# A graph network's two layers on one core: products from block 12, another order on PE and ACT, 28 early tiles

## The chip, the cores and the metric

The kernel runs on one core of a Trainium2 chip. The time is the device time of one execution in microseconds (us); the runs shown are 3 of the kernel before, 3748.28 to 3751.44 with a median of 3750.68. One more execution was taken by the hardware profiler; every row that is quoted comes from it. The engines are named as in the profile: PE multiplies matrices (PEld is its loading of weights), DVE is the vector engine, ACT the scalar engine with its table of functions, POOL the engine that issues the indirect gathers here, SP the one that issues the other DMAs.

## What is computed

A graph has 6250 nodes with 128 features and 200000 edges, sorted by their end (dst). Two layers, each added to its input:

```python
def _L0_gnn_ref(feat, src, dst, W, attn_l, attn_r, bias):
    z = (feat @ W).reshape(N, HEADS, PER_HEAD)          # 8 heads of 16
    el = jnp.einsum('nhp,hp->nh', z, attn_l)
    er = jnp.einsum('nhp,hp->nh', z, attn_r)
    e = jax.nn.leaky_relu(el[src] + er[dst], negative_slope=NEG_SLOPE)
    emax = jax.ops.segment_max(e, dst, num_segments=N)
    a = jnp.exp(e - emax[dst])
    denom = jax.ops.segment_sum(a, dst, num_segments=N)
    agg = jax.ops.segment_sum(z[src] * a[:, :, None], dst, num_segments=N)
    out = agg / jnp.maximum(denom, 1e-09)[:, :, None]
    ...

def _L1_gnn_ref(node_feats, edge_attrs, edge_feats, ...):
    s, v = ...                                          # up projections of the nodes
    h = silu(edge_feats @ A1 + b1); h = silu(h @ A2 + b2); tpw = h @ A3
    ss, vs = s[sender], v[sender]
    ...                                                 # four kinds of messages of 128 + 384 numbers
    message = jax.ops.segment_sum(mji, receiver, num_segments=num_nodes) / 10.0
    ...                                                 # output projections

h = maximum(layernorm(x), 0);  x = x + _L0_gnn_ref(h, ...)
h = maximum(layernorm(x), 0);  x = x + _L1_gnn_ref(h, ...)
```

## The kernel before

**Tiles, blocks, steps.** The edges lie in 1563 tiles of 128, the tiles in NB = 98 blocks of KB = 16 (the last has 11), each block for a window of 64 nodes. The nodes lie in NX = 50 tiles of 128. In each layer every edge needs the row of its source node out of a table in DRAM (t0, 136 numbers, for layer 0; t1, 128 numbers, for layer 1). Nearly all these rows come by indirect DMAs of POOL, one per tile of 128 edges (`gather`, L836 to L839). The exceptions:

- Column 15 of each third block comes by 128 DMAs of one row each, from SP (`rows_by_row`, L1141 to L1155); they are issued far ahead, between SP's other requests.
- Column KD = 14 of the blocks in `dense` (layer 0) or `dense1` (layer 1) is made by PE: the table lies on the chip as three bf16 parts (t0s, t1s), a one-hot matrix of the sources picks the rows by 51 products of up to 408 columns (`rows_of`, L1304), and `taken` (L1317) lays the result in place. `dense` before is blocks 21 to 93 (L1200).
- The first KX = 25 tiles of layer 0 are gathered from the raw input x while t0 is still being made (`gather_x`, L903), and put through the same arithmetic again (`rows_of` of the prologue, L938, called a second time).
- The first NE = 24 tiles of layer 1 ("early") are gathered from a copy of t1 that lacks the last three node tiles, so that POOL needn't wait for them at the seam between the layers; the missing rows are added in layer 1 by one-hot products (`late_ends`, L1863, and `late_rows`, L1877).

**The prologue** (L845 to L1005) normalizes the 50 node tiles in ten groups, multiplies by W, and writes t0. Of its subtract-and-scale operations (L960) five are given to POOL, the rest to DVE and ACT.

**Layer 0's loop** (L1577 to L1669) has one step g for each block g. PE, DVE, ACT and SP execute in the order in which the program writes their instructions, so that the order of the calls is the order of the queues. Step g works on four blocks: it ends block g−2, weights and sums block g−1 (b4), takes the logits of block g, and prepares block g+1 (n1: turning the one-hot ends, er of the ends) and g+2 (n2: one-hot ends, the products of a dense block). The calls that the change touches:

- `turned(n1, q)`, L1339: four transpositions of four one-hot tiles into p_d, which is one buffer of PSUM, and a copy d by ACT (L1348). The next turning waits for that copy.
- `er_of(n1, q)`, L1350: four small products that read d.
- `weights(b4)`, L1401: three operations of DVE, an exp on ACT (L1411), a transposition on PE (L1412), a copy on ACT (L1413). In odd steps ACT loads its function table ahead of the exp, since the node steps of even steps use a root.
- `weighted(b4, k0)`, L1416: DVE multiplies eight tiles of rows by their weights. `sums(b4, k0)`, L1425: PE adds them up by end, one product a tile, half a block a call.
- `rows_of(n2, k0, n)`: three products for each of n parts.
- `asked(k)`, L1262: SP requests three node tiles of t0 into zr, two buffers. `split(k)`, L1277: DVE makes their three parts, four operations (L1228 to L1231). Step g asks for g−2 and, at its end, splits g−3; 17 of each are needed.

The rows of block g+3 are requested in step g, and five buffers go round.

**Layer 1** (L1966 on) works in units of four tiles, 16 × 24 + 7 = 391 with the last block's 4, 4 and 3: edge network, messages, sums; then the nodes; at the end comes a tail for the last two node tiles.

Of the kernel before, what the change touches and what calls it, by code (L numbers as in the profile page):

```python
# [13 lines left out]
OP = mybir.AluOpType  # L14
# [727 lines left out]
def tile_even_edges(  # L742
# [60 lines left out]
    src_col = keep.tile([P, TU], I32, name="fsrc")  # L803
    z_first = keep.tile([P, KB, ZW], F32, name="fz_first")
    ok_i = keep.tile([1, 1], I32, name="fok")
    KX = KB + 9
    z_second = keep.tile([P, KB, ZW], F32, name="fz_second")
    other = keep.tile([P, KB, ZW], F32, name="fz_other")
    flat = other.rearrange("p k f -> p (k f)")
# [46 lines left out]
    with tc.manual_schedule(engines={mybir.EngineType.PE, mybir.EngineType.DVE,  # L856
# [81 lines left out]
        def rows_of(gx, xs, fp, fp_ps, raw=None):  # L938

            mark = "e" if raw else ""  # L940
            NC = len(gx)
            mvs, rss, mrs, hs = {}, {}, {}, {}
            todo, done, outs, ers = [], [], [], []
            for k in range(NC + 3):
                if 0 <= k - 1 < NC:
                    rss[k - 1] = deviation(fp, mvs[k - 1], gx[k - 1][1], f"x{mark}{gx[k - 1][0]}")
                c = k - 2
                if 0 <= c < NC:
                    i, n = gx[c]
                    rs, mr = rss[c], mrs[c] = normal(fp, mvs[c], rss[c], n, f"x{mark}{i}")  # L950
                    h = hs[c] = fp.tile([P, 6, P], F32, name="fh")
                    for j in range(n):
                        by = (i + j) % 7
                        if by in ((2, 6) if c < NC - 2 else (2,)):
                            nc.scalar.activation(h[:, j, :], xs[c][:, j, :], AF.Identity,
                                                 bias=mr[:, j, :], scale=rs[:, j, :])
                        else:
                            late = by in (0, 3, 5) and NC - 4 <= c < NC - 2 and not raw
                            eng = nc.gpsimd if late else nc.vector
                            eng.tensor_scalar(h[:, j, :], xs[c][:, j, :], mvs[c][:, j, 0:1],  # L960
                                              rs[:, j, :], op0=OP.subtract, op1=OP.mult)
                if k == NC + 1 and not raw:
                    uneven_edges()
                for i, n, zt in ers:
                    nc.vector.tensor_copy(er_all[:, i : i + n, :], zt[:, :n, ZW:])
                ers = []
                if k >= 3:
                    i, n = gx[k - 3]
                    zt = raw[k - 3] if raw else fp.tile([P, 6, CW], F32, name="zt", bufs=4)
                    todo += [(k - 3, zt, j0, min(3, n - j0)) for j0 in range(0, n, 3)]  # L970
                while todo:
                    c, zt, j0, m = todo.pop(0)
                    p_t = fp_ps.tile([P, 4, P], F32, name="p_t")
                    for j in range(m):
                        nc.tensor.transpose(p_t[:, j, :], hs[c][:, j0 + j, :], ident)
                    h_t = fp.tile([P, 3, P], F32, name="h_t")
                    nc.scalar.activation(h_t[:, :m], p_t[:, :m], AF.Relu)
                    done.append((c, zt, j0, m, h_t))
                    while len(done) > (1 if k < NC + 2 or todo else 0):
                        c, zt, j0, m, h_t = done.pop(0)  # L980
                        p_z = fp_ps.tile([P, 3, CW], F32, name="p_z")
                        for j in range(m):
                            nc.tensor.matmul(p_z[:, j, :], h_t[:, j, :], w_ext, start=True, stop=True)
                        outs.append((c, zt, j0, m, p_z))
                        while len(outs) > (1 if k < NC + 2 or todo or done else 0):
                            c, zt, j0, m, p_z = outs.pop(0)
                            copy = nc.scalar.copy if c < NC - 2 else nc.vector.tensor_copy
                            w = ZW if raw else CW
                            copy(zt[:, j0 : j0 + m, :w], p_z[:, :m, :w])
                            i, n = gx[c]  # L990
                            if j0 + m == n and not raw:
                                to_table(t0, zt[:, :, :ZW], i, n, nc.sync)
                                ers.append((i, n, zt))
                                load(c)
                if k < NC:
                    i, n = gx[k]
                    mvs[k] = moments(fp, xs[k], n, f"x{mark}{i}")
            for i, n, zt in ers:
                nc.vector.tensor_copy(er_all[:, i : i + n, :], zt[:, :n, ZW:])
# [11 lines left out]
def even_edges(tc, v):  # L1011
# [8 lines left out]
    with ExitStack() as ctx:  # L1020
# [25 lines left out]

        NL, NE = 3, 24
        LATE = NX - NL  # L1050
        sv_of = {}
        iota = const.tile([P, P], F32, name="fiota")
# [144 lines left out]
        order = sorted(range(NR), key=lambda k: (k > 0, 2 * NR + k < NX, k))  # L1197
        half = (NR + 1) // 2
        TS = 3
        dense = set(range(-(-NX // TS) + 4, NB - 4))  # L1200
        dense1 = set(range(10, NB - 4, 4))

        ranges = []
# [34 lines left out]
        with tc.manual_schedule(engines=in_order), \  # L1238
# [23 lines left out]
            def asked(k):  # L1262

                i = TS * k
                if 0 <= i < NX:
                    n = min(TS, NX - i)
                    zr = asked.of[k] = l0d.tile([P, TS, ZW], F32, name="zr", bufs=2)[:, :n]
                    if i == 0:
                        nc.vector.memset(zr[:W0, 0, :], 0.0)
                        nc.sync.dma_start(zr[W0:, 0, :], t0[: P - W0, :])  # L1270
                        of = t0[P - W0 : n * P - W0]
                        nc.sync.dma_start(zr[:, 1:], of.rearrange("(j p) f -> p j f", p=P))
                    else:
                        of = t0[i * P - W0 : (i + n) * P - W0]
                        nc.sync.dma_start(zr, of.rearrange("(j p) f -> p j f", p=P))

            def split(k):  # L1277
                if k in asked.of:
                    zr = asked.of.pop(k)
                    n = min(TS, NX - TS * k)  # L1280
                    in_three(t0s[:, TS * k : TS * k + n], zr, rest0[:, :n])
# [22 lines left out]
            def rows_of(c, k0, n):  # L1304

                if k0 == 0:
                    p_x = l0_ps.tile([P, 512], F32, name="p_x")
                    c["p_x"] = p_x[:, : 3 * ZW].rearrange("p (r f) -> p r f", f=ZW)
                for k in range(k0, min(k0 + n, NR)):
                    i = order[k]  # L1310
                    m = len(range(i, NX, NR))
                    for s in range(3):
                        nc.tensor.matmul(c["p_x"][:, :m, :], c["oh", k // half][:, k % half, :],  # L1313
                                         t0s[:, i::NR, s, :], start=k == 0 and s == 0,
                                         stop=k == NR - 1 and s == 2)
# [9 lines left out]
            def ends_of(c, q):  # L1325

                if 4 * q < c["kt"] and q == len(c.setdefault("s", [])):
                    c["s"].append(one_hot(c["b"] * KB + c["o"] + 4 * q, min(4, c["kt"] - 4 * q), iota_p))
# [21 lines left out]
            def er_of(c, q):  # L1350
                if 4 * q < c["kt"]:
                    b = c["b"]
                    er_w = (er3o if b % 2 else er3)[:, b // 2, :, :].rearrange("p s h -> p (s h)")
                    for k in range(min(4, c["kt"] - 4 * q)):
                        nc.tensor.matmul(er_3[:, 4 * q + k].rearrange("p s h -> p (s h)"),
                                         c["d", q][:, k, :], er_w, start=True, stop=True)
# [220 lines left out]
            for g in range(NG - 3):  # L1577
# [4 lines left out]
                    node_out(n)  # L1582
                for n in split_:
                    parts_out(n)
                asked(g - 2)
                if g % 2 == 0 and g // 2 + 2 < NX - 2:
                    node_rows(g // 2 + 2, 1)
                rows_until(rows, g + 1)
# [25 lines left out]
                er_of(n1, 0)  # L1614
                if was:
                    rows_of(n1, half + 4, NR)
                if b4:
                    weights(b4)
                if was:
                    taken(n1)  # L1620
                for n in nodes:
                    node_x(n)
                er_of(n1, 1)
                turned(n1, 2)
                if b4:
                    bank_of(b4)
                    weighted(b4, 0)
# [3 lines left out]
                er_of(n1, 2)  # L1631
                if b4:
                    weighted(b4, 8)
                if to:
                    rows_of(n2, 0, 3)
                for n in nodes:
                    node_d(n)
                    node_h(n)
                ends_of(n2, 2)
                er_of(n1, 3)  # L1640
                if b4:
                    sums(b4, 0)
                if to:
                    rows_of(n2, 3, 3)
                for n in nodes:
                    node_t(n)
                if n1 is not none:
# [6 lines left out]
                    sums(b4, 8)  # L1654
                if to:
                    rows_of(n2, 6, half - 6)
                split(g - 3)
                if g == 4:
                    ends_in_ranges(const)
                if g == NG - 4:  # L1660
# [74 lines left out]
        with tc.manual_schedule(engines=in_order), \  # L1735
# [192 lines left out]
            def dense_step(b, q):  # L1928
# [6 lines left out]
                if b in dense1:  # L1935
# [4 lines left out]
            blk = [{} for _ in range(NB)]  # L1940
            us = [{"b": b, "k0": k0, "m": min(4, KT[b] - k0)}
                  for b in range(NB) for k0 in range(0, KT[b], 4)]
            NU = len(us)

            def take_rows(b):
# [219 lines left out]
```

## Time and profile before

| | |
|---|---|
| runs: median (lowest, highest) | 3750.68 us (3748.28, 3751.44) |
| the profiled execution | 3749.37 us |
| its span, with the instructions | 3747.6 us |
| mean granted clock of PE | 0.936 |
| POOL, gathers of both layers (L839) | 2946, 0.945 us each |
| last gather from t0's table for layer 0 | block 97, ends at 1840.4 us |
| first gather from the complete t1 | 1876.60 us |
| last gather of layer 1 | ends at 3733.18 us |

How to read it: the page gives busy time by engine and by group of instructions; a timeline lists the instructions of one engine with start, duration, line, output and input, and in brackets the idle time ahead and what released it; the windows give each engine's busy time and PE's granted clock (1.00 is full speed) in a stretch. The page's chain that ended last is cut at the first steps of the end here, so that the pace of the two layers has to be read from the spacing of one line's instructions from block to block. PE's clock by fortieths of the span:

```profile
PEclk7766899999999999999799999999999999999999
```

### The profile page before, as it was taken

What the parts mean: (1) busy time and instruction counts of PE and PEld (TensorE: products, weight loads), DVE (VectorE), ACT (ScalarE), POOL (GpSimd) and SP (SyncE); (2) the same over time, 40 slices, a digit from 0 to 9 for tenths busy, and PEclk for the clock granted to TensorE, in tenths of its full rate; (3) what the DMA queues carried; (4) which work ended last, traced back from release to release, by engine and by line L of the source; (5) the groups of instructions that cost most, each with busy time, mean ns of one, the idle gap of its engine ahead of it and who ended that gap; (6) DMA issues with size and microseconds to landing.
All of it is one profiled execution on the core that took longest, in us unless ns stands there. A gap on an engine that the chain in (4) does not pass through costs nothing. (4 is left out here: it accounts for less than half of the span.)

```text
span 3747.6 us, 74803 instructions
## 1 busy us (share of the span) xinstructions
PE 3196.4 (85%) x19845; PEld 2474.1 (66%) x19845; DVE 2633.1 (70%) x6272; ACT 1406.0 (38%) x3638; POOL 2817.3 (75%) x2981
## 2 busy tenths in 40 slices
PE   4756788888888888888788899999999999999997
PEld 4655566666666666666666677777677777767775
DVE  7755666666666666666657777777777777777776
ACT  4432333333333333333334444444444444444443
POOL 7777777777777777777777777777777777777776
PEclk7766899999999999999799999999999999999999
DMA  6333332222222222222223222222222222222222
GB/s 167 75 78 79 71 68 67 68 69 68 68 68 68 68 68 67 69 69 67 71 70 95 69 64 64 64 64 64 64 64 64 65 63 64 65 63 64 63 68 52
DMA packets 212534, 262.78 MB, mean 70 GB/s; under 512 B 77425, under 2 KB 163921, under 8 KB 212097
## 3 DMA queue, kind: packets, MB, share of 16 engines
q0 software_dynamic: 95072, 200.78, 22.6%
q1 hardware_dynamic: 116592, 57.03, 5.7%
q8 instruction: 159, 2.61, 0.3%
q14 instruction: 279, 2.28, 0.2%
q10 hardware_dynamic: 432, 0.09, 0.0%
HBM read 236.19 MB, written 21.14 MB: 69 GB/s over the span
## 5 line engine op out<-in xcount | busy, mean ns | idle before, releaser
L839 POOL DMA_INDIRECT fz<-ft,fsrc x1750 | 1654.1, 945 | 539.5 <-issue 327.0
L1824 PE MATMUL p_u<-mj,s 128*128 128x256 f32 x3126 | 764.3, 388 | 87.5 <-DVE mj L1816 86.5
L1313 PE MATMUL p_x<-t0s,fz_first 128*128 128x408 bf16 (+1 forms) x3723 | 730.0, 346 | 0.0
L1824 PEld LDWEIGHTS p_u<-mj,s 128*128 128x128 f32 x3126 | 582.2, 192 | 215.6 <-DVE mj L1816 139.7
L839 POOL DMA_INDIRECT fz_other<-ft,fsrc x589 | 557.2, 946 | 179.6 <-issue 107.6
L839 POOL DMA_INDIRECT fz_second<-ft,fsrc x583 | 554.0, 950 | 178.3 <-issue 107.9
L1313 PEld LDWEIGHTS <-fz_first 128*128 128x128 bf16 x3723 | 361.5, 101 | 231.5 <-issue 17.4
L1791 ACT ACTIVATE p_w<-p_w,yb 128x64 f32<-128x64 f32 x1563 | 451.5, 289 | 117.3 <-PE p_w L1787 73.8
L1787 PE MATMUL p_w<-fa3p,h 128*128 128x256 f32 x1564 | 408.4, 384 | 0.0
L1787 PEld LDWEIGHTS p_w<-fa3p,h 128*128 128x128 f32 x1564 | 286.7, 193 | 114.5 <-issue 48.8
L1772 ACT ACTIVATE h<-p_h,fb 128x512 f32<-128x512 f32 x196 | 134.7, 687 | 585.8 <-PE p_h L1770 575.1
L1337 ACT COPY mk<-p_m 128x384 f32<-128x384 f32 (+1 forms) x99 | 47.4, 479 | 658.5 <-PE p_m L1333 651.6
L1427 PE MATMUL p_u<-fz,s 128*128 128x136 f32 x1846 | 272.9, 308 | 20.1 <-DVE fz L1422 20.1
L1427 PEld LDWEIGHTS p_u<-fz,s 128*128 128x128 f32 x1846 | 258.5, 216 | 23.8 <-DVE fz L1422 22.2
L1173 DVE TENSOR_TENSOR s<-p_i,fdloc 128x512 f32<-128x512 f32 x391 | 268.6, 687 | 3.8 <-ACT p_i L1766 3.8
L1173 DVE TENSOR_TENSOR s<-p_m,fdloc 128x512 f32<-128x512 f32 x391 | 266.2, 682 | 3.0 <-ACT mk L1337 2.7
L1770 PE MATMUL p_h<-ft,fa1p 128*128 128x128 f32 x1568 | 216.1, 282 | 56.5 <-DMA ft<-in_e_f_dram 56.3
L1770 PEld LDWEIGHTS p_h<-ft,fa1p 128*128 128x128 f32 x1568 | 208.7, 197 | 79.8 <-issue 55.7
L1348 ACT CAST d<-p_d 128x512 bf16<-128x512 f32 x391 | 229.3, 586 | 78.0 <-PE p_d L1346 34.2
L1378 DVE TENSOR_TENSOR_SCAN pe<-mk,pe 128x128 f32<-128x128 f32 x98 | 42.0, 428 | 290.8 <-PE pe L1293 271.6
L1777 ACT ACTIVATE h<-p_h,fb 128x512 f32<-128x512 f32 x196 | 134.7, 687 | 260.4 <-PE p_h L1774 260.4
L1811 DVE TENSOR_REDUCE vd<-vy 128x128 f32<-128x384 f32 x391 | 229.6, 587 | 0.0
(285 smaller groups left out, 4880.5 us busy)
## 6 DMA issues: line engine op xcount, KB each, us to landing
r<-ft SPq DMA_DIRECT2D x3968, 0.5 KB
r<-ft SPq DMA_DIRECT2D x3840, 0.5 KB
fz<-ft,fsrc POOLq DMA_INDIRECT x1750
fz_other<-ft,fsrc POOLq DMA_INDIRECT x589
fz_second<-ft,fsrc POOLq DMA_INDIRECT x583
fx<-x SPq DMA_DIRECT2D x47, 160.0 KB
ft<-in_e_f_dram SPq DMA_DIRECT2D x98, 64.0 KB
t1s<-fx SPq DMA_DIRECT2D x7, 576.0 KB
```

Source lines behind the costliest of these rows:

```text
L839: nc.gpsimd.indirect_dma_start(out=to[:, k, :width], out_offset=None, in_=table, in_offset=bass.IndirectOffsetOnAxis(ap=src_col[:, t : t + ...
L1173: nc.vector.tensor_tensor(s[:, :m], iota[:, None, :].to_broadcast([P, m, P]), dloc[:, t : t + m].unsqueeze(2).to_broadcast([P, m, P]), OP. ...
L1313: nc.tensor.matmul(c["p_x"][:, :m, :], c["oh", k // half][:, k % half, :], t0s[:, i::NR, s, :], start=k == 0 and s == 0, stop=k == NR - 1 ...
L1348: nc.scalar.copy(d[:, :m], p_d[:, :m])
L1427: nc.tensor.matmul(c["p_u"][:, :ZW], c["s"][k // 4][:, k % 4, :], c["z"][:, k, :], start=c["o"] + k == 0, stop=c["o"] + k == KT[c["b"]] - 1)
L1770: nc.tensor.matmul(p_h[:, q, :], a1p[:, q0 + q, :], c["ft"], start=True, stop=True)
L1772: nc.scalar.activation(c["h1"], p_h, AF.Silu, bias=b1)
L1777: nc.scalar.activation(h2, p_h, AF.Silu, bias=b2)
L1787: nc.tensor.matmul(w[:, k : k + n].rearrange("p k a u -> p (k a u)"), c["h2"][q // 4][:, q % 4, :], a3p[:, :n].rearrange("p k f -> p (k f) ...
L1791: nc.scalar.activation(w[:, k, ::2, :], w[:, k, ::2, :], AF.Copy, scale=c["yb"][:, k0 + k, 0:1])
L1811: nc.vector.tensor_reduce(vd, vy.rearrange("p t i u -> p t u i"), AX.X, OP.add)
L1824: nc.tensor.matmul(blk[b]["p_u"][:, :MW], u["s"][:, k, :], u["mj"][:, k, :], start=k0 + k == 0, stop=k0 + k == KT[b] - 1)
```

## The change

1. KX is KB + 13 = 29 in place of 25: four tiles more come from x, four fewer from t0.
2. All of L960's operations that POOL had go to DVE.
3. NE is 28 in place of 24.
4. `dense` begins at block 12 in place of 21.
5. Two parts of t0 are requested in each of the steps 2 to 10, and split at the end of the same step.
6. The order in a step: `er_of(n1, 1)` and `turned(n1, 2)` stand ahead of `weights(b4)`; the first three of the next dense block's parts stand ahead of `weighted(b4, 0)`, the second three ahead of the sums; the first half of the sums is parted, with `er_of(n1, 3)` between. On ACT the copy d of turning 2 so comes ahead of the table load and the exp. DVE's order is the same but for the splits.
7. The last unit of layer 1, of three tiles, becomes two of two and one.

```diff
-    KX = KB + 9
+    KX = KB + 13
...
-                            late = by in (0, 3, 5) and NC - 4 <= c < NC - 2 and not raw
-                            eng = nc.gpsimd if late else nc.vector
-                            eng.tensor_scalar(h[:, j, :], xs[c][:, j, :], mvs[c][:, j, 0:1],
-                                              rs[:, j, :], op0=OP.subtract, op1=OP.mult)
+                            nc.vector.tensor_scalar(h[:, j, :], xs[c][:, j, :], mvs[c][:, j, 0:1],
+                                                    rs[:, j, :], op0=OP.subtract, op1=OP.mult)
...
-        NL, NE = 3, 24
+        NL, NE = 3, 28
...
-        dense = set(range(-(-NX // TS) + 4, NB - 4))
+        dense = set(range(-(-NX // TS // 2) + 3, NB - 4))
...
-                asked(g - 2)
+                for k in range(2):
+                    asked(2 * g - 4 + k)
...
                 er_of(n1, 0)
                 if was:
                     rows_of(n1, half + 4, NR)
+                er_of(n1, 1)
+                turned(n1, 2)
                 if b4:
                     weights(b4)
                 if was:
                     taken(n1)
                 for n in nodes:
                     node_x(n)
-                er_of(n1, 1)
-                turned(n1, 2)
+                if to:
+                    rows_of(n2, 0, 3)
                 if b4:
                     bank_of(b4)
                     weighted(b4, 0)
...
                 er_of(n1, 2)
                 if b4:
                     weighted(b4, 8)
-                if to:
-                    rows_of(n2, 0, 3)
                 for n in nodes:
                     node_d(n)
                     node_h(n)
                 ends_of(n2, 2)
+                if to:
+                    rows_of(n2, 3, 3)
+                if b4:
+                    sums(b4, 0, 4)
                 er_of(n1, 3)
                 if b4:
-                    sums(b4, 0)
-                if to:
-                    rows_of(n2, 3, 3)
+                    sums(b4, 4, 4)
...
-                split(g - 3)
+                for k in range(2):
+                    split(2 * g - 4 + k)
...
+            if us[-1]["m"] > 2:
+                n = us[-1]["m"] - 2
+                us[-1]["m"] = 2
+                us.append({"b": NB - 1, "k0": us[-1]["k0"] + 2, "m": n})
```

## Prediction

> **What bounds the kernel now.** I read five views: the busy shares, the requests of POOL, the pace of layer 0 in PE's own order, PE's stalls in one pair of iterations (two successive blocks, 37.5 us), and the rows around the seam and the end.
>
> ```profile
> PE 3196.4 (85%) x19845; PEld 2474.1 (66%) x19845; DVE 2633.1 (70%) x6272; ACT 1406.0 (38%) x3638; POOL 2817.3 (75%) x2981
> ...
> L839 POOL DMA_INDIRECT fz<-ft,fsrc x1750 | 1654.1, 945 | 539.5 <-issue 327.0
> ```
>
> POOL is 75% busy, but each of its gathers takes 0.945 us and then 0.30 of issue, 1.2485 together, and 40 to 41 of them start in every 50 us from end to end. It never waits for a buffer. So a gather less is 1.2485 us less, wherever POOL sets the end. It pauses in two places only:
>
> ```profile
> 24.10 4.21 POOL L960 TENSOR_SCALAR fh<-fxs,mvx,rsx 128x128 f32<-128x128 f32 x5 [0.46 <-PE p_t L975]
> 28.47 1.03 POOL L905 DMA_INDIRECT fz_second<-in_e_xp_dram,frow  x1 [0.16 <-issue]
> ```
>
> ```profile
> 1869.61 0.94 POOL L839 DMA_INDIRECT fz<-ft1z,fsrc  x1 [0.31 <-issue]
> 1876.60 0.94 POOL L839 DMA_INDIRECT fz<-ft,fsrc  x1 [6.04 <-PE p_h L1868]
> ```
>
> The first is the prologue's arithmetic (next gather at 28.47 where it could be 23.94: 4.53 lost). The second is the seam: the first gather from t1 waits for layer 0's last table write, 6.04 where 0.30 is usual, 5.74 lost.
>
> PE follows the gathers in layer 0 until block 20 or so and then falls behind them: its logits come 2 us after the block's last gather at blocks 21 to 27, 27 to 30 us at 84 to 92. Its step of logits (L1372) stands at 253.25 for block 11, 429.96 for 20 and 1779.79 for 92, so (1779.79 − 429.96) / 36 = 37.50 a pair, where POOL needs 36.7 (2 × 14.67 gathers). The dense blocks, whose tile 14 PE makes itself (10.0 us of L1313 a block: 730.0 / 73), are thus bound by PE's loop, the others by POOL. Its stalls in one pair:
>
> ```profile
> 1188.54 0.33 PE L1412 MATMUL pe<-fident,a 128*128 128x128 f32 x1 [1.59 <-ACT a L1411]
> ...
> 1189.92 0.38 PE L1346 MATMUL p_d<-fidentb,s 128*128 128x128 bf16 x4 [0.73 <-ACT d L1348]
> ```
>
> ```profile
> 1207.58 0.38 PE L1346 MATMUL p_d<-fidentb,s 128*128 128x128 bf16 x4 [0.73 <-ACT d L1348]
> ...
> 1210.54 2.12 PE L1427 MATMUL p_u<-fz_other,s 128*128 128x136 f32 x16 [1.01 <-DVE fz_other L1422]
> ```
>
> In odd iterations PE waits 1.59 for the exp, because ACT loads its table first; in both 0.73 for the copy d of turned 2, since p_d is one buffer; in even ones 1.01 for DVE's weighted sums. And the clock dips:
>
> ```profile
> 1187.00:1190.40 3.40, 1.13 (x18) 0.94 (x19) 2.26 (x5) 2.33 (x5) 2.48 (x4) 1.00 0.19 44
> 1190.40:1193.80 3.40, 3.40 (x17) 2.15 (x16) 3.40 (x6) 0.58 (x1) 2.51 (x3) 0.50 0.31 70
> ```
>
> Columns: length, busy time of PE, PEld, DVE, ACT, POOL, then the granted clock. PE idles 2.27 of 3.40 us, and in the next window the clock is 0.50: nine of L1313's products take 2.78 us there, 1.54 at full clock. A dip so costs about 1.6 us, once a pair. Over all of layer 0 it follows where PE idled some 1.8 to 2.0 us or more in such a window, never below 1.6.
>
> **The change part by part.** The profiled execution took 3749.37 us (span 3747.6), 1.3 below the median of the runs, 3750.68; gains are taken from the profile and subtracted from the median.
>
> *Fewer gathers.* Dense blocks begin at 12 instead of 21: 9 × 1.2485 = 11.2 us off POOL. The five tensor_scalars go to DVE, where one takes 0.28 (1.4 in all, beside POOL's gathers): 4.5 off. Four tiles more from x and four fewer from t0 leave the number alone, but 13 gathers now end at 23.94 + 13 × 1.2485 = 40.2, near 40.8 with the delays of its neighbours (0.65 in nine), about where nine ended before (40.35), so the table's landing (40.25) still hides behind them; POOL is 3.7 to 4.5 ahead, 4.0 taken. PE and DVE pay for them in the build stage, 25 tiles in 21.3 us, 0.85 each: 3.4 later at the start, inside 13 us of slack at block 1. Were that cover gone, it would cost 3.4.
>
> *The seam.* 28 early tiles instead of 24 fill 5.0 of the 5.74.
>
> So POOL's bound on the gain is 11.2 + 4.0 + 5.0 = 20.2, up to 21.5 with the upper ends.
>
> *PE's longer stretch.* Nine more blocks have rows to make, so PE's pace counts from block 11 and not from 20. Its start is set by SP and DVE: the parts of t0 are requested (asked, L1275) two a step and split at the end of the same step, where they were split one step later. SP's requests come late among its row DMAs:
>
> ```profile
> 247.79 0.41 SPq L1275 DMA_DIRECT2D zr<-ft  x1
> ...
> 251.00 16.89 SPq L1154 DMA_DIRECT2D r<-ft  x44
> ```
>
> That is step 10's, 14 us after logits(10) at 233.95, and it lands 4 us on. The split (four DVE operations, 0.57 + 3 × 0.58 = 2.3, two of them 4.6) waits in DVE's order with everything of step g+1 queued behind: one_hot, e_s, logits. Steps 2 to 10 so end at SP's request + 4 + 4.6; by that I put logits(10) at 239 to 245 and logits(11) at 261 to 265.5, where POOL alone would allow 249. I take the late end; the lead of the gathers (41 us at blocks 6 to 17) covers POOL. Below nothing the term cannot go, since waits are only added here; at most it is 20.
>
> *The new order.* ACT now has d1, d2, table load, exp, so the exp stands behind the copy of turned 2. By hand through the rows: odd step, d2 from 1187.50 to 1188.08, load to 1189.38, exp to 1189.70, the transposition at 1189.75 where it was 1188.54; PE waits once, 2.35, in place of 1.59 + 0.73. Nothing gained, +0.1 taken. Even step (no load): the transposition moves from 1206.25 to 1207.80 behind turned 2 and d2 (a stall of 1.05), the 0.73 and the 1.01 go, since nine products stand ahead of the sums; node_t comes at 1213.6 instead of 1214.05: −0.45. A pair is then 37.50 − 0.35 = 37.15; a dip that misses its window now and then (one gap instead of several) gives another 0.1: **37.06**. What neither trace shows is what DVE makes of weights that come 1.2 to 1.5 later: between −1.0 (PE's 1.01 gone and nothing late) and +1.2 a pair (all of it handed on to e_s); I keep −0.45, the nearest row.
>
> Then logits(92) is at 265.5 + 81 × 18.53 = 1766.4, before 1779.79: 13.4 earlier. The four last blocks and the seam follow as they are: t1 lands 13.4 earlier, POOL (20.2 − 5.0 = 15.2 ahead less the four early tiles) is done 2.9 us before. From there four gathers are already made: **18.4**.
>
> *Layer 1.* Another group of early tiles must be completed by late_ends and late_rows, some 4.3 us of PE and DVE (units with them 9.3 to 11, others 5). PE starts 38 to 46 us behind the gathers and catches up by block 93; how much is left shows in DVE's waits for gathers at the end, 10 to 11 us in all, of which the largest:
>
> ```profile
> 3732.51 0.55 DVE L1807 TENSOR_TENSOR vy<-fz_other,p_i 128x384 f32<-128x384 f32 x1 [2.86 <-DMA fz_other<-ft,fsrc]
> ```
>
> PE's own end moves 13.4 − 4.3 = 9.1 and has those 11 to give: 20.1, just over POOL's 18.4. So thin a margin costs something: 1.5. Last unit split in two: DVE works 2.06 on three tiles after the last landing, then less on one, but with more fixed costs: −0.3 to +0.9, none taken.
>
> Sum: 3750.7 − (18.4 − 1.5) = **3734**. Each 0.1 us of a pair is worth 4 us.
>
> **The rivals.**
>
> *POOL bounds all along.* If the dips go, a pair takes about 35.5, under POOL's 36.7, PE stays with the gathers, and the gain is 20.2 to 21.5: **3729**. For it: one gap of 2.35 may lie across two windows; against: 2.27 idle in a window was enough at 1187, and the new gap is no smaller. The Trainium skill ("TensorE: Matmul & The Clock Gate", section "HAM oscillation — how this bites in real kernels") puts the limit at idle gaps over about 3.4 us; by that rule this rival would hold, and the trace disagrees, with 1.59 as the longest gap ahead of a dip.
>
> *The order gives nothing.* The pair stays at 37.50, because the 0.45 of even steps waits elsewhere (DVE's e_s). Then logits(92) is at 265.5 + 81 × 18.75 = 1784, 4.3 late, against 5.0 of early tiles: **3750**. For it: odd steps gain nothing by the walk.
>
> *The order costs.* Exp behind d2 makes the weights 1.2 late in odd steps, and DVE (weighted, ends_to, weighted, then one_hot and e_s without a pause: 3.40 busy of 3.40 in the window above) hands it on. If 0.6 of it survives to e_s, the pair is 37.50 − 0.35 + 0.6 = 37.75, logits(92) at 1794.4, 14.6 late, 5.0 back: **3760**. It decides from 0.35 that survives, where the pair is back at 37.50. Against it: DVE idled 1.07 before the weighted sums and e_s waits for PE's er as well.
>
> That the change does not do what it says shows as a last rival inside the second: dense blocks that bring no time, since only the bound has moved.
>
> **How the numbers follow.** Forecast (pair 36.9 to 37.3, gains of 8 to 19) 0.44; POOL-bound 0.22; nothing 0.19; costs 0.15. A measurement of this kernel tells about 0.2% (7.5 us) from no change. So faster 0.66, same 0.19, slower 0.15. The range goes from 3726 (POOL's bound with the upper ends and a little of the tail) to 3754, which takes in the second rival; the third is left out.
>
> **What would show it.** Gathers start 1.2485 apart with 9 fewer; the first gather from t1 near 1863; L1372 of block 11 near 261 to 265 and of 92 near 1766; a pair of 37.06; L1412 of odd steps after one gap of 2.35 and a dip behind it; the copy d twice ahead of the table load. Wrong would be a pair over 37.5, DVE rather than ACT ahead of PE in it, blocks 12 to 20 slower than later ones, or layer 1 that ends on DVE without waits for gathers.

## The result and the profile after

The changed kernel takes 3735.91 us (median of 6 runs, 3734.58 to 3738.26), the kernel before 3751.89 in the 6 runs that stand with it (3748.28 to 3756.64): a ratio of 0.9957, 95% interval 0.9945 to 0.9970, that is 16 us faster, 11 to 21 by the interval. The forecast was 3734. The profiled execution took 3735.78, its span is 3733.9. Eleven of the twelve executions in the experiments below were disturbed (PE, DVE, ACT and SP held up together, the kernel before at 5900 us too), and their times are only compared with each other.

The time is where it was forecast. The way there was not: what came true is the bound of the first rival, POOL from end to end, with gathers that were dearer in this execution. The same lines of the page as for before:

```profile
PE 3240.1 (87%) x20366; PEld 2486.6 (67%) x20366; DVE 2668.5 (71%) x6346; ACT 1401.8 (38%) x3643; POOL 2812.8 (75%) x2967
...
L839 POOL DMA_INDIRECT fz<-ft,fsrc x1740 | 1649.5, 948 | 530.9 <-issue 317.6
```

Ten gathers fewer stand in this group, but one takes 948 ns where it took 945. Now the two places where POOL paused. Its timeline in the prologue (start, duration, engine, line, output<-input, idle before and what ended it):

```profile
22.72 0.95 POOL L905 DMA_INDIRECT fz_first<-in_e_xp_dram,frow  x1 [0.30 <-issue]
23.98 0.98 POOL L905 DMA_INDIRECT fz_second<-in_e_xp_dram,frow  x1 [0.30 <-issue]
...
40.49 2.22 POOL L905 DMA_INDIRECT fz_second<-in_e_xp_dram,frow  x1 [0.30 <-issue]
43.02 1.79 POOL L839 DMA_INDIRECT fz_second<-ft,fsrc  x1 [0.30 <-issue]
```

and at the seam:

```profile
1863.50 0.94 POOL L839 DMA_INDIRECT fz<-ft1z,fsrc  x1 [0.30 <-PE p_h L1772]
1864.74 0.96 POOL L839 DMA_INDIRECT fz<-ft,fsrc  x1 [0.30 <-issue]
```

Both pauses are gone. The last early gather is followed by the first one from t1 after the usual 0.30, since t1's last write was issued at 1856.42 (1873.81 before). No pause of POOL is longer than 0.32 us from the first gather, at 3.81, to the end of the last, at 3719.73. The rest of the span, 14.2 us, is the tail, 14.4 before. So the whole execution can be counted in gathers. (Each row is from the timelines of POOL; the third kernel is the one of the last experiment, exp_first_24.)

| between first and last gather | before | changed | exp first, 24 early |
|---|---|---|---|
| gathers | 2971 | 2962 | 2962 |
| median duration of one, us | 0.944 | 0.947 | 0.944 |
| pauses beyond 0.305 each, sum | 10.7 | 0.4 | 0.0 |
| what gathers over 1.0 us took above the median | 8.9 | 10.4 | 6.6 |
| last gather ends | 3733.18 | 3719.73 | 3708.69 |
| span | 3747.6 | 3733.9 | 3723.1 |

From before to changed: 9 × 1.249 = 11.2 from the count and 10.3 from the pauses, 21.5 together. The others go against it: a gather is 2 to 3 ns longer all along, in layer 1 too, where both kernels gather the same, some 6.5 us (mean there, without the long ones, 0.9459 against 0.9437, times 2962), and long gathers cost 1.5 more. 21.5 − 8.0 = 13.5; the last gather ends 13.45 earlier.

PE, by its steps of logits, in two places of its timeline:

```profile
272.21 0.27 PE L1370 MATMUL pe<-fident,e_s 128*128 128x128 f32 x1
```

```profile
1756.67 0.27 PE L1370 MATMUL pe<-fident,e_s 128*128 128x128 f32 x1
```

That is blocks 11 and 92: 81 steps in 1484.5, 18.33 a step, 36.65 a pair, where 37.50 was measured before, 37.06 forecast, and POOL's pace is 36.7 to 36.8. PE's lag behind the gathers (from the end of a block's last gather to its logits), which grew from 3.5 us (block 12) to 30.5 (block 92) before, now falls slowly from 24.5 to 18.9. Within the pair the order does what the hand walk said. Counted by block, the steps with a table load are the even ones (the stall of 2.35 lies behind logits(62) at 1205.30); the description and the prediction call them odd. PE in a step without a table load and in one with:

```profile
1194.85 0.33 PE L1410 MATMUL pe<-fident,a 128*128 128x128 f32 x1 [0.94 <-ACT a L1409]
...
1214.12 0.46 PE L1410 MATMUL pe<-fident,a 128*128 128x128 f32 x1 [2.35 <-ACT a L1409]
1214.38 2.93 PE L1311 MATMUL p_x<-t0s,fz_first 128*128 128x408 bf16 x9
```

One stall each, 0.94 and 2.35, where 1.05 and 2.35 were worked out; the waits for the copy d and for DVE's sums no longer show. And ACT ahead of the stall of 2.35:

```profile
1211.86 0.59 ACT L1346 CAST d<-p_d 128x512 bf16<-128x512 f32 x1 [0.69 <-PE p_d L1344]
1212.47 1.28 ACT L1409 ACT_TABLE_LOAD   x1
1213.76 0.31 ACT L1409 ACTIVATE a<-a 128x128 f32<-128x128 f32 x1
```

The table load waits behind the copy of turning 2. The windows around it, laid on the edges of the half-clock window (length, busy PE, PEld, DVE, ACT, POOL, clock):

```profile
1210.76:1214.17 3.41, 1.06 (x13) 0.62 (x12) 1.51 (x5) 2.59 (x4) 2.66 (x3) 1.00 0.29 65
1214.17:1217.59 3.42, 3.42 (x16) 2.01 (x16) 2.67 (x3) 0.27 (x1) 2.65 (x3) 0.50 0.28 62
```

With 2.35 idle of 3.41, the next window is at half clock, and the nine products behind it take 2.93. The clock so falls as before, but not in every pair: of the 68 pairs that begin at blocks 22 to 89, 18 take 35.4 to 35.6 and 50 take 37.0 or a little more. The short ones are those in which the edge of a window cuts the gap. The step with a table load before this one, block 60:

```profile
1178.56 0.33 PE L1410 MATMUL pe<-fident,a 128*128 128x128 f32 x1 [2.35 <-ACT a L1409]
1178.73 1.55 PE L1311 MATMUL p_x<-t0s,fz_first 128*128 128x408 bf16 x9
```

```profile
1173.21:1176.62 3.41, 3.00 (x31) 1.89 (x30) 2.98 (x10) 1.33 (x4) 2.56 (x3) 1.00 0.29 62
1176.62:1180.03 3.41, 1.47 (x10) 1.03 (x11) 1.22 (x3) 2.13 (x4) 2.73 (x3) 1.00 0.28 63
1180.03:1183.45 3.42, 3.42 (x35) 2.73 (x34) 3.42 (x5) 0.59 (x1) 2.51 (x4) 1.00 0.26 58
```

The gap is the same 2.35, but 0.41 of it lies in one window and 1.94 in the next. The clock stays at 1.00, and the nine products take 1.55. There are 35 such gaps at blocks 22 to 90. In 26 of them at least 2.01 us lay in one window, and a window at half clock followed each time; in the other 9 at most 1.99 lay in one, and none followed. Each of the 9 shortens the two overlapping pairs that hold it. Why the edge comes by: a pair with a dip takes 37.0 here, half a us less than eleven windows (37.55), so that the gap moves through the windows from pair to pair. Before, such a pair took 37.4 to 37.6, and the gap kept its place: 35 dips in a row, from 439.44 to 1716.03, came 37.55 apart.

### The profile page after: what moved, and what is told of

It reads as the page before. It is cut to its first block, busy times and chain, and to the rows that moved or that the text cites. A ratio compares the mean times of both kernels' runs of the same rounds, so it can differ in the third digit from the quotient of the medians.

```text
span 3733.9 us, 76004 instructions
## 1 busy us (share of the span) xinstructions
PE 3240.1 (87%) x20366; PEld 2486.6 (67%) x20366; DVE 2668.5 (71%) x6346; ACT 1401.8 (38%) x3643; POOL 2812.8 (75%) x2967
## 5 line engine op out<-in xcount | busy, mean ns | idle before, releaser
L1311 PE MATMUL p_x<-t0s,fz_first 128*128 128x408 bf16 (+1 forms) x4182 | 817.9, 345 | 0.0
L1311 PEld LDWEIGHTS <-fz_first 128*128 128x128 bf16 x4182 | 409.6, 102 | 261.9 <-issue 28.9
L1425 PE MATMUL p_u<-fz,s 128*128 128x136 f32 x1846 | 258.4, 296 | 8.9 <-DVE fz L1420 7.8
L1425 PEld LDWEIGHTS p_u<-fz,s 128*128 128x128 f32 x1846 | 244.4, 202 | 13.4 <-DVE fz L1420 8.5
L1298 DVE TENSOR_TENSOR fz_first<-pe,place_r 128x1152 bf16<-128x1152 f32 (+1 forms) x164 | 211.1, 1287 | 27.6 <-ACT mx L1380 27.6
```

The lines of the kernel that those rows point to most:

```text
L1298: nc.vector.tensor_tensor(oh[:, :n], c["at"].unsqueeze(1).to_broadcast([P, n, P]), ranges[2][:, h * half : h * half + n].unsqueeze(2).to_b ...
L1425: nc.tensor.matmul(c["p_u"][:, :ZW], c["s"][k // 4][:, k % 4, :], c["z"][:, k, :], start=c["o"] + k == 0, stop=c["o"] + k == KT[c["b"]] - 1)
```

## The experiments

**What the disturbed executions look like.** Eleven executions, on four chips, looked like this (ACT, then PE, of the kernel before, in one step of layer 0):

```profile
2003.36 0.59 ACT L1348 CAST d<-p_d 128x512 bf16<-128x512 f32 x1 [0.53 <-PE p_er L1355]
2028.14 0.48 ACT L1337 COPY mk<-p_m 128x384 f32<-128x384 f32 x1 [24.20 <-remote]
```

```profile
2014.51 0.25 PE L1391 MATMUL pe<-mx,fshift 128*128 128x1 f32 x1
2015.44 0.16 PE L1391 MATMUL pe<-mx,fshift 128*128 128x1 f32 x1 [0.68 <-issue]
...
2029.25 0.59 PE L1396 MATMUL pe<-mx,fshift 128*128 128x1 f32 x2 [12.21 <-ACT mx L1382]
```

ACT's copy needs p_m, which PE had made by 2012.3, and starts at 2028.1; PE gets out one product in 0.7 us, SP one instruction in 0.70, until all go on at once. Single operations are as long as ever, but for PE's at a lower clock. In these executions POOL is no bound: it pauses 1800 to 2350 us in all, waiting for buffers. What they still show is the order of the waits within a step.

**before_again** is the kernel before, unchanged.

> The kernel before, once more, for one profile on the same chip as the next three. Two theories of why a gather took 0.944 us (median) in the profile of before and 0.947 in that of the changed kernel, in layer 1 too, where both execute the same: if it belongs to the execution or the chip, this profile and the next have the same median, and their spans differ by more than the 13.7 us seen so far, by 16 to 21; if it belongs to the kernel, 0.944 here and 0.947 there again, and the difference stays near 14.

5905.79. The median gather took 0.946 here and 0.944 in the changed kernel on the same chip: the other way round than in the first two profiles. So the 3 ns do not follow the change. The first theory is not met either, since it expected one median on one chip; what in an execution sets the price stays open. The spans, disturbed, say nothing on it.

**after_again** is the changed kernel, unchanged.

> The changed kernel, once more. POOL theory (requests of POOL follow each other without a pause from the first to the last, so the end is their number times their period): 16 to 21 us faster than before, with 0.30 as the largest pause in layer 0, at the seam and in layer 1. PE theory (the forecast: PE's loop sets the end of layer 0): the same time, but POOL pauses at the seam.

6079.94 against 5905.13 of before on the same chip, 1.0291 (1.0265 to 1.0318): slower, which neither theory had. Layer 0 takes the difference: from logits(12) to logits(92) 33.6 us a step where before_again has 31.6, 159 of the 171 between the two spans.

**old_order**, and **old_order_b** on another chip: turning 2, er 1, products and sums back in their old places.

```diff
-                er_of(n1, 1)
-                turned(n1, 2)
                 if b4:
                     weights(b4)
...
                 for n in nodes:
                     node_x(n)
-                if to:
-                    rows_of(n2, 0, 3)
+                er_of(n1, 1)
+                turned(n1, 2)
...
```

> The changed kernel with the old order of PE and ACT in a step (er of 1, turning 2, the products of the next dense block and the sums where they stood before); all else as changed. PE theory and POOL theory agree that PE's loop then is the slower one: pair back at 37.5 against POOL's 36.7, logits(92) at 272 + 81 x 18.75 = 1791 in place of 1757, the last table write some 29 us later, POOL pausing about 24 us at the seam: 3755 to 3762, slower than before. Rival (the order is worth nothing, only the count of gathers matters): within 3 us of the changed kernel.

> The changed kernel with the old order of PE and ACT in a step, once more, since in the first eight runs all engines paused together for 10 to 20 us at a time, in the kernel before too (5905 us), so that their times do not answer the question. If this execution is without such pauses (before near 3750): both theories, pair back at 37.5, logits(92) at 1791 in place of 1757, POOL pausing about 24 us at the seam, 3755 to 3762. Rival (the order is worth nothing): within 3 us of the changed kernel's 3736. If the pauses are there again: before near 5900 and this one within 1% of it, as in the first run.

1.0046 (1.0028 to 1.0064) and 1.0016 (0.9996 to 1.0036) of before, 31.8 us a step. Both were disturbed, so what the old order costs where POOL is the bound was not seen. But in the disturbed executions the order alone makes the 2.5% between 1.029 and 1.005. The row that carries it: from the end of DVE's subtraction to the weights' transposition on PE, median over 38 steps with a table load and 38 without, 1.62 and 1.79 in old_order, 2.94 and 2.62 in after_again. In the undisturbed profiles it is 1.61 and 0.96 before, 2.89 and 2.38 after.

**dense_21**: dense blocks from 21.

```diff
-        dense = set(range(-(-NX // TS // 2) + 3, NB - 4))
+        dense = set(range(-(-NX // TS) + 4, NB - 4))
```

> The changed kernel with dense blocks from 21 again; all else as changed, the two requests and splits a step too. POOL theory: nine gathers more, 9 x 1.25 = 11.3 us slower than the changed kernel, about 3747. PE theory: nine steps fewer with PE's products, so PE's loop is earlier by (272.2 - 253.2) less what POOL sets, the end moves by less than 5 us.

1.0255 (1.0232 to 1.0279), no slower than after_again (1.0291). Where POOL has pauses to give, nine gathers more, with nine blocks of products fewer, cost nothing. That agrees with the POOL theory's reason, but it is no test of its number.

**new_order**: the kernel before with the new order alone (the diff of old_order the other way).

> The kernel before with the new order of PE and ACT alone. POOL theory: the pair falls from 37.5 to 36.65 or less, PE's lag behind the gathers at block 92 falls from 28 us to POOL's pace, and POOL's pause at the seam (5.74) goes: 5 to 6 us faster than before, 3745 to 3747. PE theory: 72 steps x 0.42 = 30 us of PE's time, of which the seam passes on the same 5.7. Rival (exp behind the copy of turning 2 costs what the rest gains): no change.

1.0258 (1.0235 to 1.0281), 33.4 us a step: slower, which none of the three had for an undisturbed execution. With before itself (1.000), after_again and old_order this makes the four corners: new order 1.026 and 1.029, old order 1.000 and 1.005, without the other edits and with them.

**early_24**: `NL, NE = 3, 24`.

> The changed kernel with 24 early tiles in place of 28. In its profile POOL is done with 28 early tiles at 1864.4 and the last write of t1 is issued at 1856.4, landing some 2.7 later at 1859.1, so 24 would be done at 1859.4. POOL theory: no change against the changed kernel (0 to 1 us), the 28 are not needed. PE theory, and the term of the prediction: 5.0 us slower.

**old_prologue**: `KX = KB + 9`, and L960 as before.

> The changed kernel with the prologue of before: 25 tiles from x, five subtract-and-scale operations on POOL. POOL theory: POOL begins 3.7 to 4.5 us later and never makes it up, 3.7 to 4.5 slower than the changed kernel. Rival (PE's lag of 20 us hides it, as it hid 28 us before): within 1.5 us.

early_24 came to 1.0344 (1.0317 to 1.0371) of before and old_prologue to 1.0319 (1.0291 to 1.0347), where after_again stood at 1.0291 on another chip. Both were disturbed, and so there is no verdict on 5.0 and 4.0 us.

**exp_first**: table load and exp go to ACT's queue ahead of the copy of turning 2.

```diff
-                turned(n1, 2)
+                turned(n1, 2, not b4)
                 if b4:
-                    weights(b4)
+                    weights(b4, lambda: copied(n1, 2))
...
                 nc.scalar.activation(a[:kr], a[:kr], AF.Exp)
+                then()
```

> The changed kernel with one thing moved on ACT: table load and exp stand ahead of the copy of turning 2, as they did before the change, while PE keeps its new order. The exp is then earlier by 1.2 in odd steps and 0.9 to 2.0 in even ones, PE's single gap of 2.35 shrinks to about 1.1, under what was followed by a half-clock window, so a pair takes 33 to 35 without POOL. POOL theory: PE's logits then come 2 to 5 us after the block's gathers, the granted clock rises, and the time stays within 2 us of the changed kernel. PE theory: 81 x (36.65 - 34) / 2 = 107 us of PE's time, of which the end sees at least 5.

1.0093 (1.0066 to 1.0120): disturbed as well, but one copy moved on ACT takes back most of the 2.6 to 2.9%. From the subtraction to the transposition 1.62 with a table load, 2.19 without, 32.1 us a step. So it is the exp's place behind the copy, the third rival's mechanism, that costs where nothing hides it.

**after_no_rows** and **exp_first_24_no_rows** leave out SP's single-row DMAs.

```diff
             flat = table.rearrange("r f -> (r f)").bitcast(mybir.dt.uint8)
...
+            return
+            yield
...
-                nc.scalar.copy(z[:, KB - 1, :width], rows_by_row.tiles.pop((layer, b)))
+                nc.scalar.copy(z[:, KB - 1, :width], no_row[:, :width])
```

> The changed kernel without the 7808 single-row DMAs of SP: column 15 of each third block is left zero in place of its rows; everything else is as changed, gathers, products and order. In nine runs all engines paused together for 10 to 20 us at a time while SP's instructions came one per 0.70 us, and the kernel before took 5900 in them; the blocks after the last single-row DMA ran at the old pace. If the pauses hang on these DMAs they go, and the time is that of the changed kernel before them, 3728 to 3740, with no pause of POOL over 0.35 from the first gather to the last (POOL theory). PE theory: SP's freed queue lets the products start near 250 instead of 272, so logits(92) are 20 us earlier and with them the end, by 5 or more. If the pauses are of another cause, some 5900 again.

> The kernel of the run beside it with two more things changed: on ACT the table load and the exp stand ahead of the copy of turning 2, and 24 tiles are early in place of 28. POOL theory: PE's loop becomes faster by itself (its gap ahead of the weights' transposition under 1.3 us, hardly a half-clock window in layer 0), yet the end stays within 2 us of the run beside it, since POOL has no pause to lose; POOL at the seam at most 1 us. PE theory: 2 us of a pair at least, 80 us of PE's time, so 5 us or more faster from the order, and 5 slower from the four tiles; told apart by POOL's pause at the seam, which then is 5.

5784.11 and 5601.06, before on this chip 5913.89. The pauses stay without these DMAs, so my theory of them falls, and their cause stays open. Between the two, 3.2% for the exp's place and the four early tiles, once more in a regime without POOL as the bound.

**exp_first_24**: the diff of exp_first and `NE = 24`, with SP's rows. This execution was undisturbed.

> The changed kernel with two things changed: on ACT the table load and the exp stand ahead of the copy of turning 2, and 24 tiles are early in place of 28. If the execution is without the common pauses (before near 3750), POOL theory: PE's loop faster by itself (a pair bound by POOL's 36.7, few half-clock windows in layer 0), POOL's largest pause from the first gather to the last under 1.5 us, at the seam, and the end within 3 us of the changed kernel's 3736. PE theory: 5 or more faster from the order, 5 slower from the four tiles with POOL pausing 5 at the seam. If the pauses are there (before near 5900): the weights' transposition 1.6 after DVE's subtraction in steps with a table load, as in the kernel before, and 2 to 3% faster than the changed kernel, that is near before, as the first run of this ACT order was.

3725.79 (3725.03 to 3728.51, 5 runs) against 3747.53 (3741.20 to 3753.70, 8 runs) on the same chip: 0.9946 (0.9928 to 0.9964), 22 us faster than before. PE's stall at the weights, in a step without and one with a table load:

```profile
1207.48 0.28 PE L1418 MATMUL pe<-fident,a 128*128 128x128 f32 x1
...
1227.60 0.33 PE L1418 MATMUL pe<-fident,a 128*128 128x128 f32 x1 [1.09 <-ACT a L1416]
```

From 0.94 and 2.35 to nothing and 1.09. The clock from 400 to 1600 us, before, changed, and this kernel:

```profile
400.00:1600.00 1200.00, 1056.31 (x8213) 779.67 (x8211) 809.86 (x1693) 370.23 (x849) 907.74 (x959) 0.95 0.30 68
```

```profile
400.00:1600.00 1200.00, 1071.62 (x8473) 787.65 (x8472) 828.46 (x1734) 378.03 (x873) 907.72 (x957) 0.96 0.30 68
```

```profile
400.00:1600.00 1200.00, 1063.67 (x8557) 775.53 (x8556) 839.10 (x1750) 376.52 (x880) 906.93 (x962) 0.99 0.26 68
```

The half-clock windows are nearly gone, 4 in this stretch in place of 32 before and 25 in the changed kernel. PE's lag behind the gathers falls from 20.2 us at block 12 to 3.0 at block 30 and stays at 2.3 to 4.6, mostly 2.5: PE now follows the gathers. Yet the end does not move by more than the price of gathers. The page and the seam:

```profile
L839 POOL DMA_INDIRECT fz<-ft,fsrc x1744 | 1646.5, 944 | 531.8 <-issue 270.5
```

```profile
1851.19 0.94 POOL L839 DMA_INDIRECT fz<-ft1z,fsrc  x1 [0.30 <-PE p_h L1878]
1852.44 0.94 POOL L839 DMA_INDIRECT fz<-ft,fsrc  x1 [0.30 <-issue]
```

944 ns a gather in place of 948, and 24 early tiles are enough: no pause at the seam. The last gather ends 11.0 earlier than in the changed kernel's profile; 8 to 9 of that are the median's 3 ns over 2962 gathers, the rest are long gathers, 6.6 against 10.4, against which the many a little under the median count (2.1). The number of gathers is the same, and neither kernel pauses POOL. This is what the POOL theory expects of a faster PE and four early tiles fewer: nothing but the price of a gather. The number it gave (within 3 us of 3736) was missed by 10, because it had left that price out. The two kernels also ran on different chips: against before on their own chip they gain 16 and 22 us, and the intervals of the two ratios overlap. That the new place of the exp makes gathers cheaper was not tried by itself; against it stands the median of 0.944 that the changed kernel has in after_again. The PE theory, with POOL pausing 5 at the seam, falls.

## Why the prediction was right, and where it was not

- **The sum** said 16.9, measured 16.0 between the medians and 13.6 between the two profiled executions. It is right by luck, since two errors cancel: a path that was too slow by some 4.6 (21.5 that the edits brought, against 16.9), and gathers that were dearer by 8 in the profile, which no term held.
- **Fewer gathers, prologue, seam**: 11.2 + 4.0 + 5.0 was called POOL's bound. Measured 11.2, then 5.0 for the prologue's pauses (0.30 each in place of 4.83 and 0.82, the second ahead of 41.17 and not among the prediction's two places) and 5.74 for the seam, less slow gathers in the first 100 us (5.5 in place of 4.2; the longest, 1.6 to 2.3 us, each stand beside an operation of DVE of 1.8 to 1.9). The 30th gather starts at 43.02, before at 48.08: 5.1 earlier, a little more than the 3.7 to 4.5. The four tiles of the build stage did not hold POOL up, as said.
- **The start of PE's stretch**: logits(11) at 272.2, put at 261 to 265.5, late by 6.7 more. The prediction let SP's requests set it, but DVE waited for a requested part only once, 1.04 us ahead of the split at 247.00. logits(0) is already 4.7 late (88.93 for 84.25, where 3.4 was put for the build stage), and by logits(7) it is 22.8, with DVE busy for 132.8 us between logits(1) and logits(11), before 109.1. That points at DVE's own added work; it was not tried alone. It cost nothing, because of the next point.
- **The step that failed is "a dip that misses its window now and then (one gap instead of several) gives another 0.1: 37.06".** With a dip a pair takes 37.0 (37.15 by the walk), without one 35.4 to 35.6 (about 35.5 by the walk). But 18 of 68 pairs miss it, 0.26 × 1.6 = 0.42 in place of 0.1, and the pair is 36.65. That is 0.41 less, 17 us over 81 steps, and it puts PE under POOL's pace: from there the bound of the first rival holds, not the forecast. Its condition does not: 26 of the 35 dips stayed, and PE stayed some 20 us behind the gathers. Its 0.22 was too little.
- **"The four last blocks and the seam follow as they are"** failed with it. They now wait for gathers, from logits(92) to the last logits 75.9 in place of 70.2, and t1's last write is 17.4 earlier, not 13.4. By the 2.8 us from issue to POOL's next gather that before shows, it lands 5 us ahead of POOL's last early tile, so the 28 only replace others.
- **The price of the new order** was right in size (one stall of 2.35 and one near 1), and the third rival right in its mechanism: the exp is 1.28 later with a table load, 1.42 without. In the undisturbed executions the waits that went were larger; in the disturbed ones it cost 2.5%.
- **Layer 1's** 1.5 was not needed. The prediction read 10 to 11 us of DVE's waits for gathers at the end, the largest 2.86; the profile before has 17.2 from 3640 us on, the largest 3.10, so that the margin was wider. In the changed kernel they are 16.4, up to 1.93:

```profile
3682.72 0.55 DVE L1809 TENSOR_TENSOR vy<-fz,p_i 128x384 f32<-128x384 f32 x1 [1.93 <-DMA fz<-ft,fsrc]
```

- **The clock's rule.** The Trainium skill ("TensorE: Matmul & The Clock Gate", "HAM oscillation — how this bites in real kernels") speaks of idle gaps over about 3.4 us. By the windows of 3.41 us in the two profiles, all 115 at full clock with 2.0 us or more idle were followed by one at half clock, 13 of the 36 with 1.6 to 2.0 idle, and 4 of some 1750 with less than 1.4. So gaps of 2.35 do it, if one window holds 2.0 us of one. The bound of the rival that this rule fed came true all the same, for another reason: the pair no longer takes eleven windows, and in 9 of 35 steps a window's edge cuts the gap.

What stays open: the old order, 24 early tiles and the old prologue by themselves in an undisturbed execution, the cause of the pauses, and what sets the price of a gather in an execution.

## What to carry to other kernels

Count the whole run in the instructions of the engine that never waits: pauses, number and price of one, and check that they add up to the span before any other engine's pace is called the bound. Where two engines are within 2% of each other, a rare event on one of them (here a clock window) decides which is the bound, so work out how often it can occur rather than put in a small allowance. An order that adds latency to a chain is free only as long as another engine hides it; when all of them were held up, the same order cost 2.5%, and moving one copy on ACT took most of it back.

## What the runs showed of the hardware

- The same gather takes 0.944 to 0.947 us at the median from one execution to another, in either kernel; over 2962 of them the 3 ns are 9 us, 0.24% of the time.
- In the loop half clock lasts for one window of 3.41 us. It followed each of the 26 gaps that left 2.01 us or more idle in one window and none of the 9 that left at most 1.99. A loop whose period with the dip is eleven windows meets it every time (before, 37.55 us apart); one of 37.0 us misses it about once in four (9 of 35).
- In eleven executions PE, DVE and ACT stood still together, with SP's instructions 0.70 us apart meanwhile. In before_again all three were idle at once for over 3 us 98 times, 616 us in all, where the undisturbed profile of the same kernel has 8 such times and 36 us; single operations of DVE and ACT were not longer.
